# Cross-attention with a token branch: a later half sum and earlier subtractions in the last batch, value products ahead of key products in batch 0

## The chip, the cores and the metric

The kernel runs on one core of a Trainium2 chip. The metric is the device time of one launch in microseconds (us); lower is better. All data is float32.

## The reference, cut to what matters

Sixteen batches; per batch 100 queries `x` of width 640 and 722 context rows of width 384, the last 4 of which are tokens (`ca`). Eight heads of 80.

```python
query = hidden_states @ Wq
keyt = enc @ Wk                      # enc: the first 718 context rows
valt = enc @ Wv
hs = _mha(query, keyt, valt)         # softmax(q k / sqrt(80)) v, 8 heads
ca_q1 = einsum('btc,th->bch', ca, Wq_ca)[:, indices, :]   # 100 queries
ca_hs1 = _mha(ca_q1, residual, residual)                  # first softmax
ca_q2 = ca_hs1 @ Wq
ca_hs2 = _mha(ca_q2, ca @ Wk_ca, ca @ Wv_ca)              # second softmax
out = (hs + ca_hs2) @ Wout + b_out + residual
```

Three softmaxes a batch: over the 718 keys (here "the main one"), the first of the token branch, and the second, over 4 tokens.

## The kernel before, in words

**Batches.** A loop over `b` computes the scores of batch `b` (`scores`, three tiles `st[0]`, `st[1]`, `st[2]` of 120 x 2 x 800), beside that the token branch of `b` (object `now`, class `Second`), the values of `b` (`Values`, called `vv`) and the keys of `b + 1` (`Keys`, called `kk`). Then it sums the probabilities (`r_ps`, line 1408) and multiplies them with V (`a_ps`, line 1426). The output projection of a batch (`project`, line 1054) runs in the next batch; the rows of `out` that belong to the last two batches are done in the last batch and behind it.

**Values and keys in 15 products.** `V_PLAN` and `K_PLAN` form a 3 x 3 by 3 x 2 block product from 15 products instead of 18. `vv.go(n)` takes the next n products: the matmuls of one go to PSUM bank A, B, C, D or E, which is then added or copied to its place (line 439, an add on DVE, where the place was begun; line 441, a copy on ACT, where it was not). A bank keeps on accumulating: the next product into it waits until what is in it was added or copied. In the chain of banks of `V_PLAN` (A B D A B E A B C A C B A B A) the same bank often returns after one or two others. Batch 0 has no such values: `first_values` (line 409) makes them from plain blocks, three matmuls for each half.

**The main softmax.** `larger` forms the maximum over the tiles into `most`; the object `top` (class `Maximum`) turns it, reduces it (lines 706 to 718, name `mx`), spreads it (line 728, two copies on ACT, name `spread`) and turns it back (line 736, name `over`). `top.go(3)` goes up to `mx`, the next `top.go(1)` issues `spread`, the last `top.go()` issues `over`. Then `subtract(i)` takes `over` from a tile (line 1245; on DVE, and in the last batch for `st[2]` on POOL), and `exponential(i)` follows on ACT (line 1253).

**The second softmax.** `scores2` (lines 863 to 875): sum, maximum, difference on DVE, exponential on ACT. `softmax3` (881 to 883): sum and reciprocal on DVE, product on POOL into `p2_in`. `spread2` (893 to 910): a transpose on DVE (`p2t`), then a chain of DMAs from SP through HBM into `pb`. `values2` (923, 927): products and sums of `pb` on POOL into `hs2`, which `finish` adds to the last batch's result (line 1042).

**Order.** Inside the loop `manual_schedule` is on: each engine carries out its instructions in the order in which the code issues them, and waits by semaphores. An instruction that waits holds up everything behind it on its engine. So the sequence of calls in the loop's body is the schedule.

**Last batch** (`else` branch, line 1366). There are no next keys; PE has the 15 products of V, the projection of rows that batches 13 and 14 left (`project_few`, line 1079; `last.project((0,), True)`, line 1054, one half of `out`'s columns at a time), the probability sums, the second half of that projection (`last.project((1,), True)`, line 1421), the product with V, and the last rows' projection. `project` with `apart` adds the projected half to `xn` (which holds `x` plus the bias) on DVE (line 1062) and sends it out by a DMA from SP.

Of the kernel before, what the change touches and what calls it, by code (L numbers as in the profile page):

```python
# [10 lines left out]
ALU = mybir.AluOpType  # L11
# [3 lines left out]
B, S, H = 16, 100, 640  # L15
# [138 lines left out]
def kernel(  # L154
# [18 lines left out]
    nc = tc.nc  # L173
# [78 lines left out]
    def load_rest(b, enc):  # L252
        if b == 1:
            room = hsT_tile("rest_1").rearrange("p c s -> p (c s)")
            rest = room[:, : len(A_REST) * KT].rearrange("p (i k) -> p i k", k=KT)
        else:
            rest = rest_tile(f"rest_{b}")
        for (u, c), i in A_REST.items():
            nc.sync.dma_start(
                out=rest[:, i], in_=enct[b][:, c, u * (KT - 1) : u * (KT - 1) + KT]  # L260
            )
        return enc[0], rest
# [38 lines left out]
    for g in range(2):  # L301
        for c in range(CC):
            nc.scalar.dma_start(
                out=wv_sb[:, 2 * c + g],
                in_=wv[c * P : (c + 1) * P, g * (H // 2) : (g + 1) * (H // 2)],
# [21 lines left out]
    halves = [t[:, u] for t in [scores_tile(f"wq_{i}") for i in range(NP)] for u in range(2)]  # L327
# [29 lines left out]
    for h, c, r, s, k in PIECES:  # L357
        nc.gpsimd.dma_start(
            out=m2[s : s + k, c, GROUPS[c][1].index(-1), h * T : (h + 1) * T],
            in_=wqcat[h * D + r : h * D + r + k, :],  # L360
# [4 lines left out]
    for c in range(HC):  # L365
        first = c * P - HEADS[c][0] * D
        nc.gpsimd.affine_select(
            out=hmask[:, c], in_=hmask[:, c], compare_op=ALU.is_ge, fill=0.0,
# [3 lines left out]
            out=hmask[:, c], in_=hmask[:, c], compare_op=ALU.is_ge, fill=0.0,  # L372
# [29 lines left out]
    def first_values(i, enc, engines, halves=(0, 1), get=psum):  # L402

        u, j = KC[i]
        for g in halves:
            engine = engines[g]
            v_ps = get(f"v_ps_0_{i}_{g}")
            for c in range(CC):
                nc.tensor.matmul(  # L409
                    v_ps[:KN, : H // 2],  # L410
                    a_raw(enc, u, c)[:, j * KN : (j + 1) * KN],
                    wv_sb[:, 2 * c + g],
                    start=(c == 0),
                    stop=(c == CC - 1),
                )
            engine(
                vs[:, j, 2 * u + g, :, :D],
                v_ps[:KN, : H // 2].rearrange("p (h d) -> p h d", d=D),
            )
# [519 lines left out]
    class Last:  # L939


        def __init__(self, b):
            self.b = b

        def load(self, behind=None):

# [94 lines left out]
                    )  # L1041
                    nc.vector.tensor_tensor(out, out, self.hs2[:, lo:hi, cols], ALU.add)

        def project(self, halves=(0, 1), apart=False):
            for r, xn in self.xn.items():
                lo, n = OC[r]
                o_v = out.rearrange("b s n -> (b s) n")[lo : lo + n]
                if not apart:
                    both = pair(f"o_ps_{r}")
                for k in halves:  # L1050
                    cols = slice(k * (H // 2), (k + 1) * (H // 2))
                    o_ps = psumk(f"o_ps_{r}_{k}") if apart else both[:, k]
                    for c in (HC - 1, *range(HC - 1)):
                        nc.tensor.matmul(  # L1054
                            o_ps[:n, : H // 2],
                            hsTs[r][:, c, :n],
                            wout_sb[:, c, cols],
                            start=(c == HC - 1),
                            stop=(c == HC - 2),
                        )  # L1060
                    if apart:
                        nc.vector.tensor_tensor(
                            xn[:n, cols], o_ps[:n, : H // 2], xn[:n, cols], ALU.add
                        )
                        nc.sync.dma_start(out=o_v[:, cols], in_=xn[:n, cols])
                if not apart:
                    xn_v = xn[:n].rearrange("p (k d) -> p k d", k=2)
                    nc.vector.tensor_tensor(
                        xn_v, both[:n, :, : H // 2], xn_v, ALU.add
                    )  # L1070
                    nc.sync.dma_start(out=o_v, in_=xn[:n])
# [21 lines left out]
    act, dve = nc.scalar.copy, nc.vector.tensor_copy  # L1093
# [25 lines left out]
    for n, heads in enumerate(HEADS):  # L1119
        cols = len(heads) * B * T  # L1120
# [106 lines left out]
    for b in range(B):  # L1227
        p = b // 2
        e_in, now = enc, second
# [3 lines left out]
        def loads():  # L1233

            if b + 2 >= B:
                return None, None
            x_next = xT_at[0] if b % 2 else load_x(p + 1)
            xT_at[0] = x_next
            return Second(b + 2, x_next), load_enc(b + 2)
# [4 lines left out]
        def subtract(i, engine=nc.vector):  # L1244
            return engine.tensor_tensor(  # L1245
                st[i],
                st[i],
                top.over[:KN].unsqueeze(1).to_broadcast([KN, 2, ROWS]),
                ALU.subtract,
            )  # L1250

        def exponential(i):
            nc.scalar.activation(st[i], st[i], AF.Exp, scale=SCALE)  # L1253
# [28 lines left out]
        if b == 0:  # L1282
            second.scores1()
            m_next = load_m(b + 2)
            kk.go(3)
            top.go(3)
            first_values(3, e_in, (act, act), get=bank)
            top.go(1)
            kk.go(2)
            now.scores2()  # L1290
            first_values(0, e_in, (act, act), (0,), bank)
            top.go()
            kk.go(3)
            first_values(0, e_in, (act, act), (1,), bank)
            second_next, enc_next = loads()
            enc_next = load_rest(b + 2, enc_next)
            now.softmax3()
            kk.go(1)
            now.spread2()
            kk.go(1)  # L1300
            subtract(0)
            exponential(0)
            kk.go(2)
            subtract(1)
            kk.go(3)
            exponential(1)
            subtract(2)
            exponential(2)
            last_keys(b + 1, enc)
            keys(m_next)  # L1310
            enc_sums(enc_next)
            now.values2()
            second.softmax1(4)
        elif b + 1 < B:
            vv = Values(b, e_in)

            def both(n):
                vv.go(n)
                kk.go(n)

            second.scores1(seen)
            last.load(seen)
            if b + 2 < B:
                m_next = load_m(b + 2, seen)
                keys(m_next)
            if b == 1:
                load_outputs(nc.sync.dma_start, wout_sb, wout)
            top.go(3)
            both(3)
            now.scores2()  # L1330
            top.go(1)
            both(2)
            top.go()
            both(2)
            now.softmax3()
            both(1)
            now.spread2()
            vv.go(2)
            kk.go(1)
            subtract(0)  # L1340
            exponential(0)
            vv.go(1)
            last.place(subtract(1))
            last.add_bias()
            now.values2()
            vv.go(1)
            kk.go(2)
            exponential(1)
            vv.go(1)
            kk.go(2)  # L1350
            both(1)
            both(1)
            if b == 1:
                for f in list(wv_there):
                    nc.scalar.copy(wv_sb[:, W_AT[f]], wv_there.pop(f))
            if b == 1:
                nc.gpsimd.dma_start(out=bias, in_=bout[0].partition_broadcast(P))
            second_next, enc_next = loads()
            subtract(2)
            exponential(2)  # L1360
            last_keys(b + 1, enc)
            if b + 2 < B:
                enc_next = load_rest(b + 2, enc_next)
            second.softmax1()
            last.project()
        else:
            vv = Values(b, e_in)
            last.place()
            last.load()
            mine.load()  # L1370
            last.add_bias(seen)
            top.go(3)
            vv.go(3)
            last.project_few(len(OC) - 2)
            last.project((0,), True)
            now.scores2()
            top.go(1)
            vv.go(2)
            top.go()
            now.softmax3()  # L1380
            now.spread2()
            vv.go(3)
            less = subtract(0)
            exponential(0)
            wait_for(subtract(2, nc.gpsimd), less)
            now.values2()
            mine.add_bias()
            vv.go(6)
            exponential(2)
            subtract(1)  # L1390
            vv.go(1)
            exponential(1)
        if 0 < b < B - 2:
            enc_sums(enc_next)
        if b % 2 and b + 1 < B:
# [99 lines left out]
```

## Time and profile before

| | |
|---|---|
| median of 3 runs | 940.01 us (939.4 to 941.2) |
| the profiled execution: time | 939.6 us |
| its span, first to last instruction | 937.9 us |
| PE busy | 923.9 us, 99% |
| DVE / POOL / ACT busy | 640.7 / 579.6 / 375.7 us |
| mean granted TensorE clock | 0.998 |

The span is what the views below count, from 0; 1.7 us of the time lie around it. PE is busy in nearly every slice, so a place where PE stands is what to look for: `[0.70 <-DVE kT L439]` behind a row of the timeline says that the engine stood idle for 0.70 us before it, and what released it. A row of the timeline gives the start, the busy time and the instructions that it merges. A float32 matmul of the program is two passes on PE, so `x4` is two matmuls.

### The profile page before, as it was taken

Reading aid. Unit: us, or ns where it says so; the run is one execution under the profiler, and the core shown is the slowest. Engines: PE = TensorE matmul, PEld = TensorE weight load, DVE = VectorE, ACT = ScalarE, POOL = GpSimd, SP = SyncE. Lnnn points to the kernel's source line nnn. Section 1 sums busy time; section 2 is a strip of 40 time slices with the busy share of each in tenths; the row PEclk is TensorE's granted clock in tenths of the full one; section 3 lists DMA queues with packets and bytes.
Section 4 is the critical chain, followed back from the end, with each engine's and each line's share of the span. In section 5 each row is a group of like instructions: output and inputs, shape, how many; then the busy total and the mean of one; then the engine's idle time right before and its main releaser. Section 6 shows DMA issues by size and latency. Waiting matters only on the chain.

```text
span 937.9 us, 26042 instructions
## 1 busy us (share of the span) xinstructions
PE 923.9 (99%) x11183; PEld 783.3 (84%) x11183; DVE 640.7 (68%) x1087; ACT 375.7 (40%) x649; POOL 579.6 (62%) x622
## 2 busy tenths in 40 slices
PE   9999999999999999999999999999999999999987
PEld 6998879788897889888798888978889788888845
DVE  3359793967829587695946959397782958759563
ACT  2235443434334344534334344343433424444331
POOL 5849856586637856456774665758663685646434
PEclk9999999999999999999999999999999999999999
DMA  8712261150402404141321412105140150412221
GB/s 265 228 42 82 61 133 44 26 143 23 110 23 56 116 6 108 28 119 39 74 65 29 130 29 69 52 19 144 29 107 26 36 137 5 108 27 53 62 67 31
DMA packets 68667, 69.16 MB, mean 74 GB/s; under 512 B 26056, under 2 KB 62344, under 8 KB 68552
## 3 DMA queue, kind: packets, MB, share of 16 engines
q1 hardware_dynamic: 67224, 66.18, 26.5%
q8 instruction: 88, 1.44, 0.7%
q10 hardware_dynamic: 864, 0.98, 0.3%
q0 software_dynamic: 464, 0.34, 0.1%
q14 instruction: 27, 0.22, 0.1%
HBM read 61.81 MB, written 8.94 MB: 75 GB/s over the span
## 4 chain that ended last, share of the span: by engine, by line
PE 95%; DVE 3%; ACT 1%; issue 1%; DMA 0%; POOL 0%; SPq 0%; DVEq 0%; POOLq 0%; ACTq 0%
PE s_ps L643 12%; PE v_psA L468 10%; PE v_psB L468 8%; PE kT_ps L593 8%; PE k_psA L499 8%; PE a_ps L1426 7%; PE q_ps L569 7%; PE o_ps L1054 7%; PE k_psB L499 6%; PE r_ps L1408 4%; PE v_psC L468 3%; PE k_psC L499 3%; PE v_ps L409 2%; PE y_ps L782 2%; PE v_psD L468 2%; PE v_psE L468 1%
## 5 line engine op out<-in xcount | busy, mean ns | idle before, releaser
L817 POOL TENSOR_TENSOR e<-ca,g 100x800 f32<-100x800 f32 x64 | 99.3, 1562 | 153.3 <-DVE most L1257 136.3
L468 PE MATMUL v_psA<-wv_sb,enc 128*120 128x320 f32 x352 | 109.9, 435 | 0.3 <-ACT st L671 0.3
L923 POOL TENSOR_TENSOR hs<-pb,vaT 128x500 f32<-128x500 f32 x64 | 77.1, 1215 | 49.4 <-DMA pb<-wide_d 46.9
L534 POOL TENSOR_TENSOR enc<-enc 128x240 f32<-128x240 f32 x135 | 96.0, 721 | 18.0 <-ACT qp L577 10.0
L643 PE MATMUL s_ps<-qp,kT 32*120 32x100 f32 x3072 | 97.9, 263 | 0.0
L643 PEld LDWEIGHTS s_ps<-qp,kT 32*120 32x120 f32 x3072 | 95.0, 179 | 2.1 <-issue 0.2
L468 PE MATMUL v_psB<-wv_sb,enc 128*120 128x320 f32 x296 | 92.9, 436 | 0.0
L824 POOL TENSOR_TENSOR e<-e,e 100x800 f32<-100x800 f32 x48 | 90.4, 1883 | 3.8
L499 PE MATMUL k_psA<-enc,wk_sb 128*128 128x240 f32 x360 | 87.6, 366 | 0.0
L1245 DVE TENSOR_TENSOR st<-st,over 120x1600 f32<-120x1600 f32 x47 | 85.8, 1825 | 0.0
L1268 DVE TENSOR_TENSOR most<-st 120x800 f32<-120x800 f32 x16 | 17.0, 1065 | 100.1 <-ACT st L671 100.1
L468 PEld LDWEIGHTS v_psA<-wv_sb,enc 128*120 128x120 f32 x352 | 63.5, 184 | 23.4 <-DVE vs L439 0.9
L499 PEld LDWEIGHTS k_psA<-enc,wk_sb 128*128 128x128 f32 x360 | 68.3, 190 | 16.7
L1257 DVE TENSOR_TENSOR most<-most,st 120x800 f32<-120x800 f32 x64 | 65.7, 1027 | 23.2 <-ACT st L665 22.1
L1253 ACT ACTIVATE st<-st 120x1600 f32<-120x1600 f32 x48 | 73.9, 1540 | 11.1 <-DVE st L1245 9.7
L468 PEld LDWEIGHTS v_psB<-wv_sb,enc 128*120 128x120 f32 x296 | 54.7, 185 | 22.2 <-issue 0.9
L499 PE MATMUL k_psB<-enc,wk_sb 128*128 128x240 f32 x300 | 73.0, 366 | 0.0
L1027 POOL TENSOR_TENSOR hsT<-hsT,ratio 128x500 f32<-128x500 f32 (+22 forms) x26 | 20.6, 791 | 82.6 <-DVE st L1245 73.7
L1426 PE MATMUL a_ps<-st,vs 120*64 120x100 f32 (+1 forms) x1536 | 69.7, 250 | 0.5 <-issue 0.5
L927 POOL TENSOR_TENSOR hs<-hs,hs 128x500 f32<-128x500 f32 x48 | 67.3, 1402 | 3.8
L1426 PEld LDWEIGHTS a_ps<-st,vs 120*64 120x64 f32 (+1 forms) x1536 | 66.4, 137 | 3.4 <-issue 3.4
L569 PE MATMUL q_ps<-xT,wq_sb 128*128 128x200 f32 x400 | 69.1, 333 | 0.0
(166 smaller groups left out, 1845.7 us busy)
## 6 DMA issues: line engine op xcount, KB each, us to landing
pb<-p_d SPq DMA_DIRECT2D x32, 400.0 KB
enc<-in_enct SPq DMA_DIRECT2D x30, 240.0 KB
enc<-in_enct SPq DMA_DIRECT2D x15, 360.0 KB
xT<-in_xt SPq DMA_DIRECT2D x8, 500.0 KB
rest<-in_enct SPq DMA_DIRECT2D x31, 120.0 KB
xn<-in_x SPq DMA_DIRECT2D x11, 320.0 KB
wide_d<-p_d SPq DMA_DIRECT2D x16, 200.0 KB
pb<-wide_d SPq DMA_DIRECT2D x16, 200.0 KB
```

Of the source, the lines that this page charges most:

```text
L468: nc.tensor.matmul(at[0][j][:KN, : H // 2], a_form(self.enc, f)[:, j * KN : (j + 1) * KN], wv_there.get(f, wv_sb[:, W_AT[f]]), start=first ...
L499: nc.tensor.matmul(at[:, i * KT : (i + 1) * KT], wk_sb[:, W_AT[f], i], a_form(self.enc, f), start=(first and i == 0), stop=last, skip_grou ...
L534: nc.gpsimd.tensor_tensor(out, left, right, op)
L569: nc.tensor.matmul(q_ps[:, : 2 * S].rearrange("p (j s) -> p j s", j=2), wq_sb[:, c, n * P : (n + 1) * P], xT[:, :, c, :], start=(c == 0), ...
L593: nc.tensor.matmul(bank[:, i * KT : (i + 1) * KT], weights[c], a_raw(enc, u, c), start=(i == 0 and c == 0), stop=(c == CC - 1), skip_group ...
L643: nc.tensor.matmul(s_ps[bank][:n, 256 * a + lo : 256 * a + lo + rhs.shape[-1]], kT[rows, c, u, j * KN : (j + 1) * KN], rhs, start=bank not ...
L817: first = nc.gpsimd.tensor_tensor(to, self.ca[:, t, :].unsqueeze(1).to_broadcast([S, NH, S]), g[:, :, t].unsqueeze(2).to_broadcast([S, NH, ...
L824: nc.gpsimd.tensor_tensor(e, e, to, ALU.add)
L923: first = nc.gpsimd.tensor_tensor(to, pb[:, :, t], va.to_broadcast([P, HC, S]), ALU.mult)
L1245: return engine.tensor_tensor(st[i], st[i], top.over[:KN].unsqueeze(1).to_broadcast([KN, 2, ROWS]), ALU.subtract,)
L1253: nc.scalar.activation(st[i], st[i], AF.Exp, scale=SCALE)
L1426: nc.tensor.matmul(wides[64 * e : 64 * e + 64, h // 2], slot(i, h, FIRST[e], 64), st[i // 2][: KEYS[i], i % 2, h * S : (h + 1) * S], start ...
```

## The change

Two places of the loop's body are written in another order, and `project` can leave its sum for later.

- *The half projection's sum later.* `project` puts a finished half into a list `due`; `put` does the sums and the output DMAs of that list. `put=False` in the last batch leaves the first half's sum (line 1062) and its DMA until `last.put()`, which stands behind the eighth product of V.
- *Maximum spread ahead of the second softmax.* In the last batch `top.go(1)` (the copies `spread`) is issued ahead of `scores2`.
- *Subtractions first.* In the last batch the fourth to eighth products of V are not issued ahead of the first subtraction any more: `subtract(0)` stands right behind `softmax3`, ahead of `spread2` and of all adds of V; `subtract(1)` stands ahead of the adds of bank C, and `exponential(2)` ahead of the copy of the tenth product's bank.
- *Batch 0.* Both halves of `first_values(0, ...)` and the loads for batch 2 stand ahead of `scores2` and of the key products from the fourth on; the key products then follow each other without values between them.

```diff
@@ project
+        def put(self):
+            for to, o_ps, o_v in self.due:
+                nc.vector.tensor_tensor(to, o_ps, to, ALU.add)
+                nc.sync.dma_start(out=o_v, in_=to)
+            self.due = []
+
-        def project(self, halves=(0, 1), apart=False):
+        def project(self, halves=(0, 1), apart=False, put=True):
...
                     if apart:
-                        nc.vector.tensor_tensor(
-                            xn[:n, cols], o_ps[:n, : H // 2], xn[:n, cols], ALU.add
-                        )
-                        nc.sync.dma_start(out=o_v[:, cols], in_=xn[:n, cols])
+                        self.due.append((xn[:n, cols], o_ps[:n, : H // 2], o_v[:, cols]))
+                if put:
+                    self.put()
@@ batch 0
             top.go(1)
+            first_values(0, e_in, (act, act), (0, 1), bank)
+            second_next, enc_next = loads()
+            enc_next = load_rest(b + 2, enc_next)
+            now.scores2()
             kk.go(2)
-            now.scores2()
-            first_values(0, e_in, (act, act), (0,), bank)
             top.go()
             kk.go(3)
-            first_values(0, e_in, (act, act), (1,), bank)
-            second_next, enc_next = loads()
-            enc_next = load_rest(b + 2, enc_next)
             now.softmax3()
-            kk.go(1)
+            kk.go(3)
             now.spread2()
-            kk.go(1)
             subtract(0)
             exponential(0)
             kk.go(2)
@@ last batch
             last.project_few(len(OC) - 2)
-            last.project((0,), True)
+            last.project((0,), True, put=False)
+            top.go(1)
             now.scores2()
-            top.go(1)
-            vv.go(2)
             top.go()
             now.softmax3()
+            less = subtract(0)
             now.spread2()
-            vv.go(3)
-            less = subtract(0)
             exponential(0)
             wait_for(subtract(2, nc.gpsimd), less)
             now.values2()
             mine.add_bias()
-            vv.go(6)
+            vv.go(5)
+            last.put()
+            vv.go(1)
+            subtract(1)
             exponential(2)
-            subtract(1)
             vv.go(1)
             exponential(1)
+            vv.go(5)
```

Three places, as the built programs hold them. First DVE in the last batch, before, from the projection's two sums on (`xn`); `s2`, `e2`, `sm2`, `p2t` are the second softmax, `over` and `st` the main one, `vs` the values:

```order
825 L1086 TENSOR_TENSOR xn_11_9302<-o_ps_11_9333,xn_11_9302 128x320
826 L1062 TENSOR_TENSOR xn_10_9300<-o_ps_10_0_9347,xn_10_9300 128x320
827 L863 TENSOR_REDUCE s2_15_9355<-z_15_9288 100x32
...
830 L439 TENSOR_TENSOR vs_136<-v_psA_15_9293,vs_136 120x2x4x80
831 L439 TENSOR_TENSOR vs_136<-v_psB_15_9292,vs_136 120x2x4x80
832 L736 STREAM_TRANSPOSE over_15_9371<-spread_15_9362 128x800
...
835 L893 STREAM_TRANSPOSE p2t_15_9377<-p2_in_141 128x32
836 L439 TENSOR_TENSOR vs_136<-v_psE_15_0_9390,vs_136 120x4x80
...
839 L439 TENSOR_TENSOR vs_136<-v_psB_15_9292,vs_136 120x2x4x80
840 L1245 TENSOR_TENSOR st_15_0_9153<-st_15_0_9153,over_15_9371 120x1600
```

The same stretch now (lines of the program are 5 or 6 higher from the new function on: 1251 is `subtract`, 1092 and 1047 the sums):

```order
825 L1092 TENSOR_TENSOR xn_11_9302<-o_ps_11_9333,xn_11_9302 128x320
826 L863 TENSOR_REDUCE s2_15_9356<-z_15_9288 100x32
...
829 L736 STREAM_TRANSPOSE over_15_9363<-spread_15_9353 128x800
...
832 L1251 TENSOR_TENSOR st_15_0_9153<-st_15_0_9153,over_15_9363 120x1600
833 L893 STREAM_TRANSPOSE p2t_15_9370<-p2_in_141 128x32
834 L439 TENSOR_TENSOR vs_136<-v_psA_15_9293,vs_136 120x2x4x80
835 L439 TENSOR_TENSOR vs_136<-v_psB_15_9292,vs_136 120x2x4x80
...
840 L1047 TENSOR_TENSOR xn_10_9300<-o_ps_10_0_9347,xn_10_9300 128x320
841 L1251 TENSOR_TENSOR st_15_1_9201<-st_15_1_9201,over_15_9363 120x1600
842 L439 TENSOR_TENSOR vs_136<-v_psC_15_0_9417,vs_136 120x4x80
```

The first subtraction moved ahead of six adds of V, `over` ahead of two, and the half sum of `xn_10` behind all six; the second subtraction, which was the last of the stretch (row 846 before), stands ahead of bank C's adds.

Second ACT in the last batch, before and now: `spread` and `e2` are the two softmaxes, `vs<-v_ps` the copies of V's banks, `st` the exponentials.

```order
614 L875 ACTIVATE e2_15_9359<-e2_15_9359 100x32
615 L728 COPY spread_15_9362<-mx_15_9318 64x800 x2
616 L1253 ACTIVATE st_15_0_9153<-st_15_0_9153 120x1600
617 L441 COPY vs_136<-v_psC_15_0_9417 120x4x80
618 L441 COPY vs_136<-v_psC_15_1_9418 120x4x80
619 L441 COPY vs_136<-v_psA_15_9293 120x2x4x80
620 L1253 ACTIVATE st_15_2_9250<-st_15_2_9250 120x1600
```

```order
614 L728 COPY spread_15_9353<-mx_15_9318 64x800 x2
615 L875 ACTIVATE e2_15_9360<-e2_15_9360 100x32
616 L1259 ACTIVATE st_15_0_9153<-st_15_0_9153 120x1600
617 L441 COPY vs_136<-v_psC_15_0_9417 120x4x80
618 L441 COPY vs_136<-v_psC_15_1_9418 120x4x80
619 L1259 ACTIVATE st_15_2_9250<-st_15_2_9250 120x1600
620 L441 COPY vs_136<-v_psA_15_9293 120x2x4x80
```

The copies of bank C still stand behind the first exponential; the spread changed places with `e2`, and the exponential of `st[2]` with the copy of bank A.

Third PE in batch 0, a piece of the difference (`-` before, `+` now): `v_ps` are values of batch 0, `k_ps` the key products of batch 1.

```order
 L409 MATMUL v_ps_3_0_812<-wv_sb,enc_89 120x320 x3
 L409 MATMUL v_ps_3_1_817<-wv_sb,enc_89 120x320 x3
+L409 MATMUL v_ps_0_0_825<-wv_sb,enc_89 120x320 x3
+L409 MATMUL v_ps_0_1_830<-wv_sb,enc_89 120x320 x3
 L499 MATMUL k_psA_788<-enc_542,wk_sb 128x240 x2
 L499 MATMUL k_psB_792<-enc_542,wk_sb 128x240 x2
-L409 MATMUL v_ps_0_0_838<-wv_sb,enc_89 120x320 x3
 L499 MATMUL k_psA_788<-enc_542,wk_sb 128x240 x2
-L499 MATMUL k_psE_848<-enc_542,wk_sb 128x240 x2
+L499 MATMUL k_psE_864<-enc_542,wk_sb 128x240 x2
 L499 MATMUL k_psB_792<-enc_542,wk_sb 128x240 x2
-L409 MATMUL v_ps_0_1_855<-wv_sb,enc_89 120x320 x3
```

The two groups of values moved out from between the key products to ahead of them.

More of the change, by code (lines that the diff above doesn't have):

```diff
@@ L1042, in finish @@
                     nc.vector.tensor_tensor(out, out, self.hs2[:, lo:hi, cols], ALU.add)
-        def project(self, halves=(0, 1), apart=False):
+        def put(self):
+            for to, o_ps, o_v in self.due:
+                nc.vector.tensor_tensor(to, o_ps, to, ALU.add)
+                nc.sync.dma_start(out=o_v, in_=to)
+            self.due = []
+        def project(self, halves=(0, 1), apart=False, put=True):
             for r, xn in self.xn.items():
```

## The prediction

> **What bounds the kernel now.** I read the page first, then the busy time by stretch, then the timeline of the two places that are edited. The page says that PE is the bound nearly everywhere:
>
> ```profile
> PE 923.9 (99%) x11183; PEld 783.3 (84%) x11183; DVE 640.7 (68%) x1087; ACT 375.7 (40%) x649; POOL 579.6 (62%) x622
> ```
>
> So nothing is won but where PE stands. The edits touch batch 0 and the last batch alone. Two stretches of the last batch (time, busy time of PE, PEld, DVE, ACT, POOL, then granted clock, DMA share, GB/s):
>
> ```profile
> 901.40:921.06 19.66, 14.10 (x130) 8.36 (x128) 10.96 (x15) 6.54 (x7) 10.98 (x8) 0.91 0.26 64
> 908.85:913.90 5.05, 5.05 (x13) 3.17 (x14) 1.81 (x3) 2.40 (x3) 2.04 (x2) 0.66 0.74 175
> ```
>
> Of the first stretch's 19.66 us PE stands 5.56, and in the second, which lies inside it, its clock is granted at 0.66. The timeline of the last batch shows the cause, a chain through DVE and ACT:
>
> ```profile
> 893.62 0.64 DVE L718 TENSOR_REDUCE mx<-side 32x25 f32<-32x100 f32 x2
> 894.48 0.49 DVE L1086 TENSOR_TENSOR xn<-o_ps,xn 128x320 f32<-128x320 f32 x1 [0.23 <-issue]
> 897.10 1.24 PE L468 MATMUL v_psA<-wv_sb,enc 128*120 128x320 f32 x4
> 897.30 0.49 DVE L1062 TENSOR_TENSOR xn<-o_ps,xn 128x320 f32<-128x320 f32 x1 [2.33 <-PE o_ps L1054]
> 897.71 0.59 DVE L863 TENSOR_REDUCE s<-z 100x32 f32<-100x256 f32 x1
> 898.18 1.24 PE L468 MATMUL v_psB<-wv_sb,enc 128*120 128x320 f32 x4
> 898.98 1.71 ACT L728 COPY spread<-mx 64x800 f32<-64x800 f32 x2
> 900.72 1.01 DVE L736 STREAM_TRANSPOSE over<-spread 128x800 f32<-128x800 f32 x1 [0.31 <-ACT spread L728]
> 901.41 1.24 PE L468 MATMUL v_psB<-wv_sb,enc 128*120 128x320 f32 x4
> 902.20 0.24 POOL L883 TENSOR_TENSOR p_in<-e,sm 100x32 f32<-100x32 f32 x1 [8.05 <-DVE sm L882]
> 902.48 0.21 DVE L893 STREAM_TRANSPOSE p2t<-p_in 128x32 f32<-128x32 f32 x1 [0.45 <-POOL p_in L883]
> 902.61 0.84 DVE L439 TENSOR_TENSOR vs<-v_psE,vs 120x320 f32<-120x320 f32 x2
> 903.12 1.34 PE L468 MATMUL v_psC<-wv_sb,enc 128*120 128x320 f32 x4 [0.47 <-DVE vs L439]
> 903.56 0.82 DVE L439 TENSOR_TENSOR vs<-v_psA,vs 120x640 f32<-120x640 f32 x1
> 905.03 1.81 DVE L1245 TENSOR_TENSOR st<-st,over 120x1600 f32<-120x1600 f32 x1
> 906.94 1.54 ACT L1253 ACTIVATE st<-st 120x1600 f32<-120x1600 f32 x1 [6.26 <-DVE st L1245]
> 906.99 3.57 POOL L1245 TENSOR_TENSOR st<-st,over 120x1600 f32<-120x1600 f32 x1 [4.55 <-DVE st L1245]
> 908.39 0.73 ACT L441 COPY vs<-v_psC 120x320 f32<-120x320 f32 x2
> 908.85 1.81 PE L468 MATMUL v_psC<-wv_sb,enc 128*120 128x320 f32 x4 [3.07 <-ACT vs L441]
> 915.88 2.72 DVE L1245 TENSOR_TENSOR st<-st,over 120x1600 f32<-120x1600 f32 x1
> 916.27 2.08 PE L1408 MATMUL r_ps<-st,vs 120*32 120x100 f32 x64
> 918.64 1.54 ACT L1253 ACTIVATE st<-st 120x1600 f32<-120x1600 f32 x1 [1.57 <-DVE st L1245]
> 920.23 0.90 PE L1408 MATMUL r_ps<-st,vs 120*32 120x100 f32 x32 [1.88 <-ACT st L1253]
> 921.06 2.96 PE L1054 MATMUL o_ps<-wout_sb,hsT 128*128 128x320 f32 x10
> ```
>
> `mx` is done at 894.26, but `spread` starts at 898.98, because on ACT it stands behind the second softmax's exponential, which on DVE stands behind the half sum, which waits for PE until 897.30. So `over` ends at 901.73 and, behind the adds of V, the first subtraction at 906.84. The copy of bank C on ACT stands behind the first exponential: PE idles 3.07 us for it. The second subtraction stands last on DVE, and the probability sums idle 1.88 us for its exponential.
>
> **The last batch, step by step.** Without the half sum, DVE goes from L1086 (ends 894.97) through `scores2` to about 896.0. `spread` starts right at `mx`'s end: 894.3 + 1.71 = 896.05. `over` takes 1.01: 897.1. Two small operations of `softmax3`, 0.4: 897.45. First subtraction, 1.81: 899.25, against 906.84. It releases the first exponential on ACT (to 900.8), and on POOL, behind `p_in`, the subtraction of `st[2]`, 3.57: 903.1. On DVE `p2t` stands behind the subtraction and waits for POOL's `p_in` (0.24), which is ready to run at 897.5, while DVE subtracts. If the two run side by side, `p2t` starts at 899.2; if POOL is held until DVE is done, at 899.5; it was 902.48. The row above with 2.72 us beside POOL's sums, against 1.81 alone, speaks for the second, and I take it. The Trainium skill, "SBUF — State Buffer", section "Who interferes with whom", says the same as a rule: a DVE instruction with two SBUF inputs and a POOL instruction that reads SBUF lock each other out, and the first to start keeps the port to its end. By that rule the sum is as below, without it 0.3 less.
>
> Now what waits behind it on DVE: six adds of V, then the half sum (0.49), then the second subtraction. The adds start at 899.4 to 899.7: A 0.82, B 0.82, both halves of E 0.84. PE's next group into bank A is due at 897.10 + 3 x 1.08 = 900.34 (1.08 a group, by the rows at 897.10 and 898.18) and needs the first add, which ends at 900.2 to 900.5: 0 to 0.3 us lost, new. Bank C's first group needs E's add, there by 902.1, before it is due: the 0.47 goes. The next adds of A and B end by 903.7, the half sum at 904.1, the second subtraction at 905.9, against 918.60. Both copies of C are through on ACT by 904.4, since PE's group starts at 902.6 and takes 1.34, and the first exponential has ended long before: the 3.07 goes. Next on ACT: the exponential of `st[2]`, to 905.9, then the copy of A, 0.69, to 906.5; PE needs that bank at 901.6 + 5 x 1.08 = 907.0. Half a microsecond is left there, the thinnest cover of the plan. The last exponential ends at 907.9, before the sums begin: the 1.88 goes.
>
> PE then has, from 901.41 on, eight groups: B, C, A, C, B, A, B, A, 8 x 1.08 = 8.6, ending 910.0. With 0.3 for the late add the sums start at 910.3. Undisturbed they last 2.21 (batch 14's, from 872.92 to the next product):
>
> ```profile
> 872.92 2.28 PE L1408 MATMUL r_ps<-st,vs 120*32 120x100 f32 x96
> 875.13 4.15 PEld L1426 LDWEIGHTS a_ps<-st,vs 120*64 120x64 f32 x96 [0.15 <-issue]
> 917.12 1.01 PEld L1408 LDWEIGHTS r_ps<-st,vs 120*32 120x32 f32 x44 [0.36 <-ACT vs L441]
> ```
>
> and, as in before (last row), they wait for the copy of the last bank A, with its pipeline some 0.5. So `o_ps` starts at 913.0 instead of 921.06: **8.0 us less**. Of these the named idle times are 0.47 + 3.07 + 1.88 = 5.4, and the slow clock 1.8: the stretch at 0.66 took 5.05 for three groups, which at full clock take 3.2. The rest is the refilling of the pipeline at each wait.
>
> The slow clock came once, behind a stand of 3.07 us. The Trainium skill, "TensorE: Matmul & The Clock Gate", section "Part 1: The HAM clock gate", says that the clock falls to half after about one idle window of 3.4 us, free-running. Here 3.07 us sufficed, so the measurement decides. By that rule alone the 1.8 us would not have been there to win, and the gain would be 6.2.
>
> **Whether the end follows by 8.0.** From `o_ps` on the order is the same. One thing comes from elsewhere: `hs2` on POOL, fed by the DMAs behind `p2t`.
>
> ```profile
> 913.58 2.02 POOL L923 TENSOR_TENSOR hs<-pb,vaT 128x500 f32<-128x500 f32 x2 [3.02 <-DMA pb<-wide_d]
> 915.68 1.25 POOL L927 TENSOR_TENSOR hs<-hs,hs 128x500 f32<-128x500 f32 x1
> 917.01 2.49 POOL L923 TENSOR_TENSOR hs<-pb,vaT 128x500 f32<-128x500 f32 x1
> 923.95 4.34 PE L1426 MATMUL a_ps<-st,vs 120*64 120x100 f32 x96
> ```
>
> From `p2t`'s start to POOL's first product lie 11.1 us, so POOL starts at 910.6, only 3 us earlier. Four products of 1.01 and three sums of 1.25 with their gaps are 8.3: done by 918.9. It is needed when the product with V ends, 928.29 - 8.0 = 920.3. It still fits, with 1.4 us of 5 left.
>
> The product of 2.49 lay beside DVE's subtraction of 2.72; alone they take 1.01 and 1.81. In the new order the second subtraction starts at 904.1, POOL's ends at 903.1 and its products start at 910.3, so nothing of that kind is paid.
>
> The half sum at nothing: its PSUM bank is next taken by the last projection, its DMA has no reader, and on SP it now stands behind the DMAs to `pb`.
>
> **Batch 0.** Its timeline has one wait of PE:
>
> ```profile
> 74.65 0.97 PE L499 MATMUL k_psA<-enc,wk_sb 128*128 128x240 f32 x4
> 75.46 0.97 PE L499 MATMUL k_psB<-enc,wk_sb 128*128 128x240 f32 x4
> 85.33 0.65 DVE L439 TENSOR_TENSOR kT<-k_psC,kT 128x480 f32<-128x480 f32 x1
> 86.03 1.08 PE L499 MATMUL k_psC<-enc,wk_sb 128*128 128x240 f32 x4 [0.70 <-DVE kT L439]
> ```
>
> With the refill that wait costs 0.86. In the new order it goes, since C's add stands ahead of the subtraction, but others come. A key group takes 0.81; a bank that returns after one other group is due 1.62 after its start, and its end (0.97), its add (0.65) and two signals take 1.82: 0.2 lost. Values no longer lie between, so that happens at three places (A B A, B A B, C A C): 0.6. Then a group A whose add stands behind the first subtraction: 0.97 + about 1.7 of the subtraction + 0.65 + 0.1 = 3.4 against 2.65 until the bank is due: 0.8. DVE is behind by that, so the last exponential is late for the sums by about 0.3. Together 1.7, less 0.86: **0.9 us more**. Bounds: 0 if DVE's adds find the gaps, 2.5 if the last two terms double. The loads moved ahead cost nothing: they wait for PE's last read of the old buffer, which comes 4 us sooner.
>
> **Sum.** -8.0 + 0.9 = -7.1. The profiled execution took 939.6 (span 937.9, and 1.7 around it), which becomes 932.5; it lies 0.4 under the median of 940.01. On the median: **932.9 us**.
>
> **The rivals.**
>
> *The copy of bank A comes late (10%).* If DVE runs 0.7 us behind my times before POOL's subtraction starts, or POOL's ends beside DVE's second one, `exponential(2)` ends 1 to 2 us later and the cover of 0.5 is gone: 1 to 3 us back, 934 to 936. For it: thin cover. Against it: 1.0 us between POOL's end and DVE's start.
>
> *`hs2` comes late (7%).* If the DMAs take over 1.4 us longer, the end waits for POOL: 0.5 to 2 us, 933.4 to 935.
>
> *Batch 0 loses its upper bound (8%).* 2.5 instead of 0.9, 934.5; POOL's products there could hold DVE's small operations, as 1.26 us for one that takes 0.19 in the last batch shows.
>
> ```profile
> 78.45 1.26 DVE L872 TENSOR_TENSOR e<-s,mx 100x32 f32<-100x32 f32 x1
> 898.55 0.19 DVE L872 TENSOR_TENSOR e<-s,mx 100x32 f32<-100x32 f32 x1
> ```
>
> *The change does not do what it says (4%).* A stand of the old size turns up at another bank and, with the slow clock behind it, eats the gain: within 0.2% of 940, 1.9 us, about what a measurement of this kernel can tell from no change.
>
> *Slower (3%).* All adds of V now queue on DVE behind `p2t`, which waits for POOL's small product, and so does PE's next group into A. Each us that `p2t` is late past 899.7 PE stands a us, and past some 3 us the clock halves for another 1.8. To lose 1.9 beyond 940, PE would have to stand 7.2 us more: `p2t` at 906.9. By the row of `p_in`, POOL had stood idle 8.05 us before it, and I see nothing that would hold it; 942 then.
>
> **How the numbers follow.** The likeliest case has the remaining 68%. The range takes in its own bounds (gain of 8.0 +/- 1, loss of 0 to 2.5) and the rivals up to 936: **931.4 to 936.0**, with some 15% outside. Faster by over 0.2%: 68 + 10 + 7 + 8 = 93%; within: 4%; slower: 3%.
>
> **What would show it.** In the profile after: `spread` within 0.1 of `mx`'s end; the first subtraction of the last batch ending ahead of the fourth add of V; no wait of PE over 0.6 us in the last 50 us before `o_ps`, and the clock at 1.00 there; `hs2` done before the product with V ends; in batch 0 four or five waits of PE of 0.04 to 0.7 us. I am wrong if a wait of over 1 us stands at bank A or C, if the clock still drops, or if batch 0 ends more than 2.5 us later.

## The result, and the profile after

The changed kernel takes 933.67 us (median of 6 runs, 933.57 to 934.31), the kernel before 940.55 us beside it (6 runs, 939.4 to 941.74): a ratio of 0.9928, 95% interval 0.9915 to 0.9941, or 5.5 to 8.0 us less. Forecast were 932.9 us and 7.1 us less. One run of before beside the experiments below took 1196.46 us at a mean clock of 0.753, far from all others, and is left out of every comparison. The profiled execution took 933.61 us with a span of 931.9, and PE stays the bound (the page's line of busy times):

```profile
PE 923.7 (99%) x11183; PEld 784.3 (84%) x11183; DVE 650.8 (70%) x1087; ACT 375.4 (40%) x649; POOL 573.3 (62%) x622
```

The two profiled spans differ by 6.0 us. To see where, I take stretches between the same events in both, from the timeline. Before: batch 0 from the first key product of bank A to the first product with V, then the start of the last batch and its last projection (the product with V at 923.95 and `o_ps` at 921.06 are shown in the prediction):

```profile
68.96 1.00 PE L499 MATMUL k_psA<-enc,wk_sb 128*128 128x240 f32 x4
...
94.52 3.31 PE L1426 MATMUL a_ps<-st,vs 120*64 120x100 f32 x72
...
887.02 0.75 PE L844 MATMUL z_ps<-y,e 100*32 100x33 f32 x64
...
928.22 6.05 PE L1054 MATMUL o_ps<-wout_sb,spare 128*128 128x320 f32 x20
```

After, the first three of these (the rest stands further below):

```profile
69.51 1.00 PE L499 MATMUL k_psA<-enc,wk_sb 128*128 128x240 f32 x4
...
96.50 3.75 PE L1431 MATMUL a_ps<-st,vs 120*64 120x100 f32 x82
...
888.87 0.75 PE L844 MATMUL z_ps<-y,e 100*32 100x33 f32 x64
```

| stretch | before | after | difference | forecast |
|---|---|---|---|---|
| batch 0: `k_psA` to `a_ps` | 25.56 | 26.99 | +1.43 | +0.9 |
| last batch: `z_ps` to `o_ps` | 34.04 | 25.86 | -8.18 | -8.0 |
| `a_ps` to the last `o_ps` | 4.27 | 4.64 | +0.37 | 0 |

These three add up to -6.38. The first product comes 0.55 us later than in the profile of before, though the edits do not touch what lies ahead of it, and the stretches between and behind are 0.17 us shorter together; that makes the 6.0.

**The last batch.** The stretch that answers to the 19.66 us shown before, from the third group into bank B to `o_ps` (time, busy time of PE, PEld, DVE, ACT, POOL, granted clock, DMA share, GB/s):

```profile
903.16:914.73 11.57, 11.43 (x129) 7.72 (x127) 7.41 (x11) 5.00 (x6) 3.73 (x4) 1.00 0.52 122
```

PE stands 0.14 us in it instead of 5.56, at full clock. The timeline after:

```profile
895.38 0.66 DVE L718 TENSOR_REDUCE mx<-side 32x25 f32<-32x100 f32 x2
896.07 1.73 ACT L728 COPY spread<-mx 64x800 f32<-64x800 f32 x2 [2.32 <-DVE mx L718]
899.06 1.77 DVE L1251 TENSOR_TENSOR st<-st,over 120x1600 f32<-120x1600 f32 x1
899.31 1.62 POOL L883 TENSOR_TENSOR p_in<-e,sm 100x32 f32<-100x32 f32 x1 [3.40 <-DVE sm L882]
900.97 0.21 DVE L893 STREAM_TRANSPOSE p2t<-p_in 128x32 f32<-128x32 f32 x1
901.01 1.24 PE L468 MATMUL v_psE<-wv_sb,enc 128*120 128x320 f32 x4
901.10 0.78 DVE L439 TENSOR_TENSOR vs<-v_psA,vs 120x640 f32<-120x640 f32 x1
902.09 1.24 PE L468 MATMUL v_psA<-wv_sb,enc 128*120 128x320 f32 x4
905.18 0.48 DVE L1047 TENSOR_TENSOR xn<-o_ps,xn 128x320 f32<-128x320 f32 x1
905.58 1.81 DVE L1251 TENSOR_TENSOR st<-st,over 120x1600 f32<-120x1600 f32 x1
907.28 0.68 ACT L441 COPY vs<-v_psA 120x640 f32<-120x640 f32 x1
908.55 1.24 PE L468 MATMUL v_psA<-wv_sb,enc 128*120 128x320 f32 x4
912.03 2.77 PE L1413 MATMUL r_ps<-st,vs 120*32 120x100 f32 x96
914.73 2.96 PE L1061 MATMUL o_ps<-wout_sb,hsT 128*128 128x320 f32 x10
```

`spread` follows `mx` at once, the first subtraction runs ahead of all adds of V, and no group of V waits long for its bank: the third group into A starts 1.08 us behind E's, the step of an undisturbed row, and only the last one into A, at 910.80, comes 0.09 us late. The probability sums run through in one row.

**The end.** Here a wait is new (POOL, DVE and PE, from POOL's first product for `hs2` on):

```profile
912.33 2.03 POOL L923 TENSOR_TENSOR hs<-pb,vaT 128x500 f32<-128x500 f32 x2 [7.76 <-DMA pb<-wide_d]
...
917.62 4.34 PE L1431 MATMUL a_ps<-st,vs 120*64 120x100 f32 x96
...
919.35 1.24 POOL L927 TENSOR_TENSOR hs<-hs,hs 128x500 f32<-128x500 f32 x1
920.56 1.53 POOL L966 TENSOR_TENSOR spare<-spare,bias 128x640 f32<-128x640 f32 x1
920.63 1.58 DVE L1043 TENSOR_TENSOR spare<-spare,hs 128x100 f32<-128x100 f32 x1 [2.24 <-POOL hs L927]
922.26 6.03 PE L1061 MATMUL o_ps<-wout_sb,spare 128*128 128x320 f32 x20 [0.30 <-DVE spare L1043]
```

`hs2` is ready in time, but POOL's next operation, the sum of the bias, starts at the same moment as DVE's small sum, and that one takes 1.58 us.

**Batch 0.** The first subtraction and what lies beside it, before:

```profile
83.63 1.78 DVE L1245 TENSOR_TENSOR st<-st,over 120x1600 f32<-120x1600 f32 x1
...
87.31 1.71 POOL L534 TENSOR_TENSOR enc<-enc 128x240 f32<-128x240 f32 x1 [0.89 <-DMA enc<-in_enct]
```

After; ahead of the subtraction stand a key group into bank B and the next one into bank A, which had been used just before B:

```profile
79.24 0.97 PE L499 MATMUL k_psB<-enc,wk_sb 128*128 128x240 f32 x4
80.32 1.05 PE L499 MATMUL k_psA<-enc,wk_sb 128*128 128x240 f32 x4
...
85.56 0.97 PE L499 MATMUL k_psA<-enc,wk_sb 128*128 128x240 f32 x4
85.75 0.69 POOL L534 TENSOR_TENSOR enc<-enc 128x240 f32<-128x240 f32 x1
...
86.53 2.25 DVE L1251 TENSOR_TENSOR st<-st,over 120x1600 f32<-120x1600 f32 x1
...
88.70 0.65 DVE L439 TENSOR_TENSOR kT<-k_psA,kT 128x480 f32<-128x480 f32 x1
89.40 1.08 PE L499 MATMUL k_psA<-enc,wk_sb 128*128 128x240 f32 x4 [0.97 <-DVE kT L439]
```

A bank that returns so soon costs 0.27 us here (1.08 from group to group instead of 0.81; its add on DVE ended at 80.17). The large wait is at bank A, 0.97 us, behind a subtraction that takes 2.25 us; POOL's sums for the batch after next, which in before waited for their load until 87.31, now run at 85.75.

### The profile page after: what moved, and what is told of

The parts are those of the page before. It is cut to its first block, busy times and chain, and to the rows that moved or that the text cites. A ratio compares the mean times of both kernels' runs of the same rounds, so it can differ in the third digit from the quotient of the medians.

```text
span 931.9 us, 26041 instructions
## 1 busy us (share of the span) xinstructions
PE 923.7 (99%) x11183; PEld 784.3 (84%) x11183; DVE 650.8 (70%) x1087; ACT 375.4 (40%) x649; POOL 573.3 (62%) x622
## 4 chain that ended last, share of the span: by engine, by line
PE 96%; DVE 2%; DMA 1%; issue 0%; ACT 0%; POOL 0%; SPq 0%; DVEq 0%; ACTq 0%
PE s_ps L643 12%; PE v_psA L468 10%; PE v_psB L468 8%; PE kT_ps L593 8%; PE k_psA L499 7%; PE q_ps L569 7%; PE a_ps L1431 7%; PE o_ps L1061 7%; PE k_psB L499 6%; PE r_ps L1413 4%; PE v_psC L468 3%; PE k_psC L499 3%; PE v_ps L409 2%; PE y_ps L782 2%; PE v_psD L468 2%; PE v_psE L468 2%
## 5 line engine op out<-in xcount | busy, mean ns | idle before, releaser
L923 POOL TENSOR_TENSOR hs<-pb,vaT 128x500 f32<-128x500 f32 x64 | 73.0, 1150 | 53.7 <-DMA pb<-wide_d 51.2
```

Of the source, the lines that this page charges most:

```text
L923: first = nc.gpsimd.tensor_tensor(to, pb[:, :, t], va.to_broadcast([P, HC, S]), ALU.mult)
```

## The experiments

Seven kernels ran, each timed in five rounds. Before had medians of 940.8 us in the runs beside the last batch's and the bias kernels (the first four below) and 940.64 us beside the other three.

| kernel | us | ratio to before, 95% interval | batch 0, `k_psA` to `a_ps` | last batch, `z_ps` to `o_ps` |
|---|---|---|---|---|
| last batch alone | 932.64 | 0.9913, 0.9891 to 0.9935 | 25.77 | 25.96 |
| sum and spread alone | 939.73 | 0.9987, 0.9972 to 1.0001 | 25.39 | 32.61 |
| subtractions alone | 939.86 | 0.9993, 0.998 to 1.0006 | 25.57 | 32.14 |
| bias first | 933.69 | 0.9921, 0.9902 to 0.9941 | 27.00 | 26.30 |
| batch 0 alone | 941.63 | 1.0009, 0.9994 to 1.0024 | 26.99 | 34.36 |
| enc sums later | 933.78 | 0.9925, 0.9906 to 0.9943 | 26.79 | 25.86 |
| last batch alone, bias first | 932.52 | 0.9913, 0.9894 to 0.9931 | 25.41 | 25.95 |

The last two columns are from one profiled execution each, like the table above. The medians tell 7 us well, but 0.3 us not at all; steps of that size are read from the traces.

**The last batch alone.** The changed kernel with the calls of batch 0 in the old order:

```diff
-            first_values(0, e_in, (act, act), (0, 1), bank)
-            second_next, enc_next = loads()
-            enc_next = load_rest(b + 2, enc_next)
-            now.scores2()
             kk.go(2)
+            now.scores2()
+            first_values(0, e_in, (act, act), (0,), bank)
...
```

> The change with batch 0 written as before: only the last batch is new. Theory (batch 0 costs the time that the trace shows between its first key product and the product with V, 27.0 against 25.6 us): 1.4 us faster than the change, near 932.3, with the wait of 0.70 at k_psC back and those of 0.97 and four small ones gone. Rival (the difference in batch 0 is the scatter of the start of a run, and all of the 6.9 us are the last batch's net gain): within 0.4 of the change, 933.3 to 934.1.

```profile
69.62 1.00 PE L499 MATMUL k_psA<-enc,wk_sb 128*128 128x240 f32 x4
...
95.39 3.31 PE L1433 MATMUL a_ps<-st,vs 120*64 120x100 f32 x72
```

932.64 us; batch 0 takes 25.77 us, 1.22 less than changed, and the last batch keeps its gain (25.96). So the edit of batch 0 is a loss. By the medians alone it would not be settled: the intervals of the two ratios overlap. But the four profiles with the edit (changed, bias first, batch 0 alone, enc sums later) have 26.79 to 27.00 us there, the five without it 25.39 to 25.77.

**Batch 0 alone.** The kernel before with the other side of the same edit.

> The kernel before with the change of batch 0 alone. Theory: batch 0 loses 1.2 to 1.4 us. From the first key product of bank A to the first product with V 27.0 us instead of 25.6; PE waits 0.9 to 1.0 us for bank A's add behind the first subtraction, which takes 2.25 us beside POOL's enc sums, and the wait of 0.7 at bank C is gone; last batch as before, with its stand of 3.07 us and the half clock; the median 1.3 us over before's. Rival (the loss is the 0.9 that was forecast, and the rest of what was seen is scatter between two executions): 26.4 us there, 0.9 us over before.

The timeline of batch 0, then two rows and the windows of the last batch:

```profile
86.13 2.25 DVE L1245 TENSOR_TENSOR st<-st,over 120x1600 f32<-120x1600 f32 x1
...
89.01 1.08 PE L499 MATMUL k_psA<-enc,wk_sb 128*128 128x240 f32 x4 [0.97 <-DVE kT L439]
```

```profile
910.74 2.49 PE L468 MATMUL v_psC<-wv_sb,enc 128*120 128x320 f32 x4 [3.07 <-ACT vs L441]
...
919.04 1.87 DVE L1245 TENSOR_TENSOR st<-st,over 120x1600 f32<-120x1600 f32 x1
...
905.00:910.00 5.00, 2.67 (x8) 1.30 (x8) 3.64 (x4) 1.16 (x1) 1.11 (x1) 0.99 0.14 34
910.00:915.00 5.00, 4.26 (x8) 2.71 (x9) 0.98 (x2) 3.15 (x5) 2.46 (x1) 0.50 0.92 213
915.00:920.00 5.00, 5.00 (x33) 2.83 (x31) 3.35 (x4) 0.47 (x1) 3.95 (x4) 0.83 0.00 1
```

26.99 us in batch 0, as in the changed kernel, with the same 2.25 and 0.97: the loss of 1.43 is the edit's, not scatter. The excess over before, 0.8 us by the ratio, has an interval from -0.6 to 2.3 and settles nothing. The windows are of interest for the clock: it was at 0.50 from 910 and still below 1 past 915, some 6.8 us in all (0.1 ahead of 910, by the mean of 0.99 there; 5.0; and 1.7 of the next 5, whose mean is 0.83). That is twice as long as in before.

**Enc sums later.** The changed kernel; POOL's first sum for the batch after next waits, in batch 0, for the first subtraction:

```diff
+            made = nc.gpsimd.tensor_tensor(out, left, right, op)
+            if behind is not None:
+                wait_for(made, behind)
+                behind = None
...
-            subtract(0)
+            behind = subtract(0)
...
-            enc_sums(enc_next)
+            enc_sums(enc_next, behind)
```

> The changed kernel; in batch 0 POOL's first enc sum waits for the first subtraction on DVE (in the changed kernel it started 0.8 us ahead of it, since the load of its rows was moved 3.5 us forward). Theory: the subtraction takes 1.78 us instead of 2.25, PE waits 0.5 instead of 0.97 us for bank A, batch 0 is 0.4 to 0.5 us shorter (26.5 instead of 27.0 from the first key product of bank A to the first product with V): median 933.2; POOL's products for hs2 start some 2.5 us later and nobody waits for them. Rival (the subtraction is long for another reason, or the second subtraction then pays what the first saves): 27.0 there, 933.7.

```profile
86.23 1.78 DVE L1254 TENSOR_TENSOR st<-st,over 120x1600 f32<-120x1600 f32 x1
...
88.64 1.08 PE L499 MATMUL k_psA<-enc,wk_sb 128*128 128x240 f32 x4 [0.50 <-DVE kT L439]
...
89.06 2.12 DVE L1254 TENSOR_TENSOR st<-st,over 120x1600 f32<-120x1600 f32 x1
...
95.17 0.90 PE L1416 MATMUL r_ps<-st,vs 119*32 119x100 f32 x32 [0.29 <-ACT st L1262]
```

Both were right in part. The subtraction is back at 1.78 us and the wait at bank A at 0.50, so POOL's sums were what lengthened it. But the second subtraction now pays (2.12 instead of 1.84 in the changed kernel), the probability sums wait 0.29 us for the last exponential, and of the 0.47 us 0.20 are left (26.79). The median, 933.78, does not show it.

**Bias first.** The changed kernel with `mine.add_bias()` issued ahead of `now.values2()` in the last batch:

```diff
-            now.values2()
             mine.add_bias()
+            now.values2()
```

> The change with POOL's bias sum of the last rows issued ahead of its products for hs2 instead of behind them. Theory (that sum, 1.53 us, held the port while DVE's small sum of hs2 wanted it, so DVE took 1.58 for 0.26 and PE waited 0.30 for it): DVE's sum takes 0.3, PE's wait of 0.30 goes, 0.3 to 0.4 us faster than the change, near 933.3. Rival (PE's wait comes from hs2 itself, late by the DMAs): no change or a later hs2, 933.6 to 934.5.

```profile
917.37 4.34 PE L1431 MATMUL a_ps<-st,vs 120*64 120x100 f32 x96
...
921.28 0.26 DVE L1043 TENSOR_TENSOR spare<-spare,hs 128x100 f32<-128x100 f32 x1 [2.35 <-POOL hs L927]
921.64 6.05 PE L1061 MATMUL o_ps<-wout_sb,spare 128*128 128x320 f32 x20
```

DVE's sum takes 0.26 us again, PE's wait is gone, and `a_ps` to the last `o_ps` is back at 4.27. That shows the cause of the 0.37 us. The median (933.69) does not resolve it, and DVE now waits for `hs2` itself until 921.28, so that its sum ends 0.1 us before PE starts. The bias sum now lies beside the second subtraction, which takes 2.17 us instead of 1.81; nobody waits for that. From `z_ps` to `o_ps` this execution took 0.44 us more than the changed kernel, 0.23 of it at the third group into A, which started 1.31 us behind E's: there the first add of V came late, for which the prediction had allowed 0.3. The edit does not touch what lies ahead of that.

**Sum and spread alone.** The kernel before, with the half sum behind the eighth product of V and `top.go(1)` ahead of `scores2`; the subtractions stay where they were.

```diff
-            last.project((0,), True)
-            now.scores2()
+            last.project((0,), True, put=False)
             top.go(1)
+            now.scores2()
...
+            last.put()
             vv.go(6)
```

> Batch 0 as before; in the last batch only the half sum later and the spread of the maximum ahead of the second softmax, the subtractions where they were. Theory (each part alone leaves another wait in its place): the spread starts at the maximum's end, over 2 us earlier, but the first subtraction still stands behind adds that wait for PE, so it comes at most 0.7 us earlier; the wait of about 3 us at bank C and the halved clock stay; 0.5 to 1 us faster than before, near 939.7. Rival (the half sum was the whole cause): 932 to 934.

```profile
904.91 1.82 DVE L1251 TENSOR_TENSOR st<-st,over 120x1600 f32<-120x1600 f32 x1
...
908.72 1.70 PE L468 MATMUL v_psC<-wv_sb,enc 128*120 128x320 f32 x4 [3.07 <-ACT vs L441]
```

939.73 us, 0.13% under before (interval 0.28% less to 0.01% more). `spread` starts early, but the subtraction stands behind DVE's adds until 904.91, and the copy of bank C behind its exponential: the stand of 3.07 us is there unchanged, as expected.

**Subtractions alone.** The kernel before with the first subtraction ahead of the adds of V and the second ahead of bank C's; sum and spread stay where they were.

```diff
-            vv.go(2)
             top.go()
             now.softmax3()
+            less = subtract(0)
             now.spread2()
-            vv.go(3)
-            less = subtract(0)
...
```

> Batch 0 as before; in the last batch only the subtractions first, the half sum and the order of spread and second softmax as before. Theory: over comes as late as before, near 901.7 on the clock of the profile before, and now six adds of V stand behind it, so PE stands about 4 us at its second product into bank A, with the clock halved behind it; later waits go. 2 us faster than before from the waits, near 938.5 (937.5 to 940 with the slow clock). Rival (the subtractions' place was the whole cause): 932 to 934.

The timeline's row of PE, then the window around it:

```profile
906.73 2.49 PE L468 MATMUL v_psA<-wv_sb,enc 128*120 128x320 f32 x4 [4.34 <-DVE vs L439]
```

```profile
905.00:910.00 5.00, 3.27 (x6) 2.09 (x7) 3.90 (x7) 1.54 (x1) 4.31 (x2) 0.66 0.02 3
```

939.86 us, no difference that can be told (1.9 us less to 0.6 more); of the 2 us that were expected, 1.90 show in the trace alone. The adds stand behind a subtraction that still waits for the late `spread`; the stand moves from bank C to bank A, grows to 4.34 us, and the slow clock follows it. In the traces the two halves gain 1.43 and 1.90 us from `z_ps` to `o_ps`, together they gain 8.18: a PE wait goes only when the whole chain to the subtraction and the queue behind it are early.

**Last batch alone, bias first.** Both edits that had shown a gain in the trace, together; I took it for the best version.

> The changed kernel with batch 0 as before and POOL's bias sum ahead of its products for hs2. Theory: both small losses go, the bank waits of batch 0 and the 0.30 us of PE at the very end: 1.2 + 0.3 under the changed kernel, about 932.2; the first sum of the last rows on DVE takes 0.26 us instead of 1.58, and from the product with V to the end 10.86 us. Rival (hs2 is done later by the bias sum's 0.3 us and now ends last): no wait at the projection, but DVE stands for hs2 instead and the end is no earlier than with batch 0 undone alone, 932.6.

```profile
920.75 0.26 DVE L1043 TENSOR_TENSOR spare<-spare,hs 128x100 f32<-128x100 f32 x1 [3.57 <-POOL hs L927]
921.07 5.86 PE L1061 MATMUL o_ps<-wout_sb,spare 128*128 128x320 f32 x20 [0.31 <-DVE spare L1043]
```

932.52 us, the lowest median, but not to be told from 932.64. Here the rival was right in its outcome, not in its reason: DVE's sum is short, but it waits for `hs2`, whose DMAs came later in this execution (12.7 us from `p2t` to POOL's first product, 11.36 in the changed kernel), while the bias sum had ended long before. Bias first took 12.3 us for the same chain and the subtractions alone 12.15, the others 11.1 to 11.5; no run shows why. The wait of 0.31 us stands in the old place with another cause.

## Why the prediction was right, and where it was off

933.67 us lie inside the range of 931.4 to 936.0. That 6.9 us less came so near to the 7.1 is in part luck: the three stretches of the profiles add up to -6.38, since two losses were larger than forecast, and the medians differ by more than the stretches.

**The last batch, forecast -8.0, measured -8.18.** The chain came as worked out, 1.78 us later on the clock of this profile (`mx` ends at 896.04 instead of 894.26). Taken from `mx`'s end: `spread` at 0.03, the end of the first subtraction at 4.79 (forecast 4.99), `p2t` at 4.93 (5.24), the second subtraction at 9.54 (9.84), the sums at 15.99 (16.04), `o_ps` at 18.69 (18.74). That both the idle times and the slow clock would go together was the step on which the 8 us rested, and the two kernels with half of the edit, which lose the gain with the stand, show it.

**`p2t` held by the subtraction, right in kind.** `p_in` took 1.62 us beside DVE's subtraction, 0.24 in before, and ended 0.1 behind it, so POOL was held, as I had taken it. But `p2t` started 0.14 us behind the subtraction's end, between the two values that I had weighed (at once, or 0.25 later). That its 4.93 lies beside the 4.94 of the value not taken is chance, since the subtraction ended 0.2 us early. The rule of the Trainium skill, "SBUF — State Buffer", section "Who interferes with whom", agrees with the row of `p_in`, and with the two kernels that moved POOL's operation away.

**The thin cover at bank A, forecast 0.5, measured 0.6.** The copy ends at 907.96 and PE takes the bank at 908.55, without a wait. The rival of a late copy did not come.

**The half sum at nothing, held.** It runs at 905.18, and no engine waits for its result.

**The end follows by 8.0: off by 0.37.** `hs2` was done at 920.59, which is 24.55 us behind `mx`, forecast 24.64, with 1.4 us to spare as forecast. The step that failed came after it: I counted POOL's products and left out the sum of the bias that stands behind them in POOL's queue. In before it ran from 923.22 to 924.77 and DVE's sum came behind it at 924.99, 3 us ahead of PE's need; now both start when `hs2` is done, and 1.4 us do not hold the two. That was shown by moving it.

**Batch 0, forecast +0.9, measured +1.43.** The returning banks cost 0.2 to 0.3 us each, as forecast, and the first subtraction did delay bank A. Mis-sized was that term: from group to group 3.84 us (85.56 to 89.40) instead of 3.4, against 2.65 that are free, so 1.2 instead of 0.8, since the subtraction took 2.25 us where 1.78 stood in before. The step behind it that failed was "the loads moved ahead cost nothing". I had asked only what the loads wait for, not what they release: POOL's sums started before the subtraction. With them out of the way the wait was 0.50. POOL did hold DVE, as the rival of the upper bound had it, but the subtraction and not a small operation. One sign that I had named failed with it: PE waits 0.97 us at one place in batch 0, where at most 0.7 were to come. The last exponential was late for the sums by 0.2 to 0.3, as forecast. Within the bounds of 0 to 2.5 the mechanism held.

**The slow clock, forecast 1.8 us of the gain.** Before, both half edits and batch 0 alone have a stand of 3.07 or 4.34 us and each has the half clock behind it; the changed kernel and the four others without such a stand have none ahead of the end. What the clock was worth apart from the stand was not measured; 3.4 us at half, as in before, are 1.7 us of work at full clock. In before it fell at 909.6, 3.8 us after PE began to stand; in batch 0 alone at 909.9, 2.2 us after (the stand began at 907.67). The window rule of the Trainium skill ("TensorE: Matmul & The Clock Gate", "Part 1: The HAM clock gate"), about 3.4 us of idleness, would have left 1.8 us of the gain out; these runs speak against taking it as a threshold for a single stand. The 3.07 us of before would not decide that alone, since the ends of matmuls are modelled and the weight loads stood 3.58 us at the same place; the fall after 2.2 us (2.7 by the weight loads) does.

**Slips in the working.** 894.3 + 1.71 is 896.0, not 896.05, and POOL's first product is put at 910.6 in one place and at 910.3 in another; neither moves the 8.0. The lower end of the range, 931.4, lies above the 931.0 that a gain of 9.0 and no loss would give.

## What to carry to other kernels

A chain that is late for two reasons gives little until both are gone (1.43 and 1.90 us here, 8.18 together): follow it from the waiting engine back to the first operation that could have run, and price the edit as a whole. When a load or a result comes earlier, ask what it starts on an engine beside which the one being hurried takes longer (2.25 us instead of 1.78 here), and read the queue of each engine one operation further than the result that is needed. Where half clock follows a stand, as here, the stand costs more than its own time.

## What the runs showed of the hardware that was not expected

- **Small operations pay the partner's whole length.** A product of 0.24 us on POOL took 1.62 beside DVE's subtraction; a sum of 0.26 us on DVE took 1.58 beside POOL's bias sum of 1.53. In either case the later one ended within about 0.1 us of the earlier one.
- **The half clock does not last the same in every run.** It followed the stand of 3.07 us for 3.4 us in the profile of before, and the same stand for 6.8 us in that of batch 0 alone. The runs of before go with it: of 39 runs beside the experiments, the 12 with a mean clock of 0.995 or 0.996 have a median of 943.0 us, the 4 with 0.997 of 941.1, the 15 with 0.998 of 940.6, the 8 with 0.999 or more of 938.5. None, one or two stretches of 3.4 us at half clock would give such mean clocks, but those runs have no trace that shows it, and what such a stretch costs in time is open (next point). The changed kernel's six runs have a clock of 0.999 or 1.0 and lie within 0.8 us.
- **The longer half clock cost little in that profile, by the order of two operations.** With 6.8 us at half clock the stretch from `z_ps` to `o_ps` took 34.36 us, with 3.4 us 34.04: PE's wait for the last exponential behind it shrank from 1.88 to 1.02 us. The subtraction ahead of that exponential took 1.87 us instead of 2.72. In before it started at 915.88, 1.05 us ahead of the end of POOL's sum for `hs2`; here, later by the clock, at 919.04, 0.2 us ahead of the end of that sum (917.99, 1.24 us). So no run shows that the second half of the 6.8 us is cheap by itself.
